# Preparing a graph layer's weights: W1 slices turned one ahead, a few loads moved forward, and part of the products given to GpSimd

## The chip, the cores and the metric

The kernel runs on one core of a Trainium2 chip. A core has five engines that run their own instruction lists in order and wait for one another by semaphores: TensorE (PE, matrix products; its weight loads are shown apart as PEld), VectorE (DVE), ScalarE (ACT), GpSimd (POOL) and SyncE (SP), which here only starts transfers. Transfers (DMA) are started from the lists of SP, ACT and POOL. The metric is the device time of one execution in microseconds (us), taken as the median of several runs.

## The reference, cut to what matters

The program is one block over 1250 rows of 768 numbers: a graph attention layer, a linear attention and a mixture of experts. The change touches only the way in which the weights of the graph layer are prepared. What is computed there:

```
x_norm = layer_norm(layernorm(x), norm_g, norm_b)      # 1250 x 768
h1     = x_norm @ W1                                   # W1: 768 x (4 heads x 192)
s_src1 = (h1 * a_src1).sum(-1);  s_dst1 = (h1 * a_dst1).sum(-1)
out1   = softmax-weighted sum of h1 over the edges, per head, + b1
h2     = out1 @ W2                                     # W2: 768 x (2 heads x 96)
s_src2 = (h2 * a_src2).sum(-1);  s_dst2 = (h2 * a_dst2).sum(-1)
```

All of it is linear between the two softmaxes, so the kernel multiplies the weights together first. `w2x` holds W2 with extra columns: W2 times `a_src2` and times `a_dst2`, summed per head, and the values of `a_src1` and `a_dst1`. `wg` is diag(norm_g) W1 times `w2x`, head by head; `bw` is norm_b W1 times `w2x`. The rows of the graph then only have to be multiplied by `wg`.

## The kernel before, in words

The part in question is the first of the program, and everything else follows it. It is written in one function, `gps_block`, in the pools named ph1.

**Loads.** SP starts W2 (`w2`, L164), W1 in three pieces of two slices each (`w1s`, L170), then `wub` and the edge ends (`ends_i`). POOL starts the ten tiles of x (`acc`, L175); nine of them are held behind the second piece of W1 by a dependency written out by hand (L177). ACT starts the small vectors: four loads into `rb` (L190), `ra` (L191), the two rows of `a2` spread over 96 partitions (L193, L194), `nbb` (norm_b spread likewise, L196), `br` and `sgb`. Each transfer signals one of a few semaphores; a load that takes one whose former load is under way waits for it to land.

**Small transposes.** `turned` (L202) turns `rb` and `ra` on TensorE and copies them out on ACT (`bc`, `gb`).

**w2x** (L213 to L225) on VectorE: it is cleared, W2 is copied in (L216), and for j = 0 (a_src2) and j = 1 (a_dst2) the product of W2 and the spread row is taken in two halves of 96 x 768 (`pr`, L221) and summed along the rows into `w2x` (L224). Two small copies put columns of `bc` in (L225).

**The slices of W1** (loop of L230 over KD = 6 slices k): eight transposes (L235, `p_w1` in PSUM, four to a bank), two copies to `wt` on ACT (L236; two buffers), a product of `wt` with norm_b on VectorE (`wb1`, L238; one buffer) and its sum into a column of `bw1` (L239), the products of `wt` with `w2x` on TensorE (L244) and the eviction to `wg` on ACT, scaled by `gb` (L246).

**After the loop**: the sum `bws` (L249), the products for `bw` (L254), for `bias` (L264, L266) and `b1w2` (L271); the layer norm's statistics of the first tiles (`norm(0)`: `moments`, L141 to L144, and `rsqrt`, L126 to L131); the edge ends are cast on POOL (`ends_f`, L283), turned on TensorE (`pe`, L287) and made into tables on VectorE (`src_f`, `hi`, `lo`, `key`, `rel`, L289 to L301).

**The stage behind it** (L318 to L420) counts edges and multiplies the tiles by `wg`: VectorE writes one-hot tables (`los`, L374; `wide`, L377), TensorE multiplies them (`pc`, L387), and in between turns the normalised rows (`pt`, L406) and multiplies them by `wg` (`ph`, L411). POOL adds `bias` to `acc` (L402).

**What sets the order.** The text is not the order of execution. The build's planner takes the instructions of all engines, with their dependencies and its own idea of durations, and writes one fixed list for each engine; on the chip each engine works its list strictly in order. So layer norm instructions of L141 to L155 and L401 stand among those of the weights on VectorE's list, and which comes first is decided when the program is built. The rotating buffers (`bufs=`) of a pool add waits: a tile's next write waits for the readers of the one it replaces.

Of the kernel before, what the change touches and what calls it, by code (L numbers as in the profile page):

```python
# [8 lines left out]
F32 = mybir.dt.float32  # L9
# [10 lines left out]
P = 128  # L20
# [4 lines left out]
KD = D // P  # L25
# [5 lines left out]
H1, C1 = 4, 192  # L31
H2, C2 = 2, 96
# [17 lines left out]
CO = H2 * (C2 + 1) + 2 * H2  # L50
# [5 lines left out]
def part_bcast(ap, parts, n):  # L56

    return bass.AP(tensor=ap.tensor, offset=ap.offset, ap=[[0, parts], [1, n]])
# [3 lines left out]
def gps_block(ctx: ExitStack, tc: tile.TileContext, x, src, dst, norm_g, norm_b, W1, a_src1, a_dst1, b1,  # L62
              W2, a_src2, a_dst2, b2, Wu, bu, w_qkv, w_proj, b_proj, router_w, w_gate, w_up, w_down,
              ws_gate, ws_up, ws_down, sg_w, sg_b, out):
    nc = tc.nc
# [14 lines left out]
    ident = const.tile([P, P], F32, name="ident")  # L80
# [80 lines left out]
    with tc.tile_pool(name="ph1", bufs=1, reuse_waits="tile") as p1, tc.tile_pool(name="ph1w", bufs=2, reuse_waits="tile") as p1w, \  # L161
            tc.tile_pool(name="ph1ps", bufs=2, space=PSUM, reuse_waits="tile") as ps:
        w2 = p1.tile([C2, 2 * H1, H2 * C2], F32, name="w2")
# [3 lines left out]
        w1s, w1d = [], []  # L167
# [15 lines left out]
        nc.sync.dma_start(ends_i[:, 1, :], dst.rearrange("(r e) -> r e", e=2 * TP))  # L183


        ra = p1.tile([KD, P], F32, name="ra")
        rb = p1.tile([3 * 2 * H1 + H2, C2], F32, name="rb")
        for i, (v, n) in enumerate(((b1, 8), (a_src1, 8), (a_dst1, 8), (b2, 2))):
            v = v if len(v.shape) == 1 else v.rearrange("h c -> (h c)")
            nc.scalar.dma_start(rb[8 * i:8 * i + n, :], v.rearrange("(k p) -> k p", p=C2))  # L190
        nc.scalar.dma_start(ra[0:KD, :], norm_g.rearrange("(k p) -> k p", p=P))  # L191
        a2 = p1.tile([C2, 2, H2 * C2], F32, name="a2")
        nc.scalar.dma_start(a2[:, 0, :], part_bcast(a_src2, C2, H2 * C2))  # L193
        nc.scalar.dma_start(a2[:, 1, :], part_bcast(a_dst2, C2, H2 * C2))  # L194
        nbb = p1.tile([C2, D], F32, name="nbb")
        nc.scalar.dma_start(nbb, part_bcast(norm_b, C2, D))  # L196
        br = p1.tile([2, D], F32, name="br")
        nc.scalar.dma_start(br[0:1, :], bu.rearrange("(o d) -> o d", o=1))
        nc.scalar.dma_start(br[1:2, :], b_proj.rearrange("(o d) -> o d", o=1))
        nc.scalar.dma_start(sgb, part_bcast(sg_b, TP, 1))  # L200

        def turned(rows, n, w, name):  # L202
            pt = ps.tile([P, 4, P], F32, name=f"p_{name}", tag="tr")
            nc.tensor.transpose(pt[:w, 0, :n], rows, ident[:n, :n])
            c = p1.tile([w, n], F32, name=name)
            nc.scalar.copy(c, pt[:w, 0, :n])
            return c

        bc = turned(rb, 3 * 2 * H1 + H2, C2, "bc")
        gb = turned(ra, KD, P, "gb")  # L210


        w2x = p1.tile([C2, 2 * H1, CG], F32, name="w2x")  # L213
# [3 lines left out]
        for j in range(2):  # L217
            o = H2 * (C2 + 1) + j * H2
            for k0 in range(0, 2 * H1, 4):
                pr = p1w.tile([C2, 4, H2, C2], F32, name="pr")  # L220
                nc.vector.tensor_mul(pr, w2[:, k0:k0 + 4].rearrange("p k (h c) -> p k h c", h=H2),  # L221
                                     a2[:, j, :].rearrange("p (h c) -> p h c", h=H2)[:, None].to_broadcast(
                                         [C2, 4, H2, C2]))
                nc.vector.tensor_reduce(w2x[:, k0:k0 + 4, o:o + H2], pr, axis=AX.X, op=ALU.add)  # L224
            nc.vector.tensor_copy(w2x[:, :, CO + j], bc[:, 8 * (j + 1):8 * (j + 2)])  # L225

        bw1 = p1.tile([C2, KD, 2 * H1], F32, name="bw1")
        for k in range(KD):  # L230
            wt = p1w.tile([C2, 2 * H1, P], F32, name="wt")
            for j0 in range(0, 2 * H1, 4):
                pt = ps.tile([P, 4, P], F32, name="p_w1", tag="tr")
                for j in range(4):
                    nc.tensor.transpose(pt[:C2, j, :], w1s[k][:, (j0 + j) * C2:(j0 + j + 1) * C2], ident)  # L235
                nc.scalar.copy(wt[:, j0:j0 + 4, :], pt[:C2, :, :])  # L236
            wb1 = p1w.tile([C2, 2 * H1, P], F32, name="wb1", bufs=1)
            nc.vector.tensor_mul(wb1, wt, nbb[:, None, k * P:(k + 1) * P].to_broadcast([C2, 2 * H1, P]))  # L238
            nc.vector.tensor_reduce(bw1[:, k, :], wb1, axis=AX.X, op=ALU.add)  # L239
            pm = ps.tile([P, 2, 512], F32, name="p_wg", tag="mm", bufs=3)  # L240
            for h in range(H1):
                o = (h % 2) * CG
                for i in range(2):
                    nc.tensor.matmul(pm[:, h // 2, o:o + CG], wt[:, 2 * h + i, :], w2x[:, 2 * h + i, :],  # L244
                                     start=(i == 0), stop=(i == 1))
            nc.scalar.activation(wg[:, k, :].rearrange("p (s c) -> p s c", s=2), pm[:, :, :2 * CG], AF.Copy,  # L246
                                 scale=gb[:, k:k + 1])
        bws = p1.tile([C2, 2 * H1], F32, name="bws")
        nc.vector.tensor_reduce(bws, bw1.rearrange("p k j -> p j k"), axis=AX.X, op=ALU.add)  # L249
        pb = ps.tile([TP, 2, 512], F32, name="pb", tag="mm", bufs=3)  # L250
# [67 lines left out]
    with tc.tile_pool(name="cnt", bufs=1, reuse_waits="tile") as cp, \  # L318
# [74 lines left out]
        for t0 in range(0, NT, 2):  # L393
# [4 lines left out]
            for i, t in enumerate(ts):  # L398
# [4 lines left out]
                for k0 in range(0, KD, 3):  # L403
                    pt = ps.tile([P, 4, P], F32, name="pt", tag="tr")
# [94 lines left out]
    with tc.tile_pool(name="ph2", bufs=1, reuse_waits="tile") as p2:  # L499
# [14 lines left out]
        with tc.tile_pool(name="kvw", bufs=2, side="right", reuse_waits="tile") as p2w, tc.tile_pool(name="kvps", bufs=2, space=PSUM, reuse_waits="tile") as ps:  # L514
# [5 lines left out]
            for pr in range(0, NPAIR, 2):  # L520

                wkv = wkv0
                if pr > 0:
                    wkv = (p2w if pr == 2 else early).tile([P, KD, 2, 2 * P], F32, name=f"wkv{pr}", bufs=1,
                                                           tag="wkv" if pr == 2 else "early")
# [280 lines left out]
    with tc.tile_pool(name="fln", bufs=2, reuse_waits="tile") as pw, tc.tile_pool(name="flnps", bufs=2, space=PSUM, reuse_waits="tile") as ps:  # L806
# [40 lines left out]
        for r in range(2):  # L847
# [5 lines left out]
            f = pw.tile([TP, NT], F32, name=f"r_f{r}", bufs=1)  # L853
# [310 lines left out]
```

## Time and profile before

| | |
|---|---|
| median of 3 runs | 1597.15 us (1594.57 to 1598.87) |
| the profiled execution: its own time | 1597.16 us |
| its span | 1595.1 us |
| granted TensorE clock, mean | 0.985 of full speed |
| busy: PE, PEld | 1525.0 us (96%), 855.7 us (54%) |
| busy: DVE, ACT, POOL | 724.4 us (45%), 367.6 us (23%), 98.1 us (6%) |
| first product of w2x and a W1 slice (L244) starts | 17.71 us |
| first product of the counting stage (L387) starts | 59.62 us |

How to read the views. The timeline has one line for each group of equal instructions in a row: start, busy time, engine, source line, operation, output<-inputs, partitions x elements, count, and in square brackets how long the engine had been idle before and what ended that. Waits are listed as waiting engine and line, what it waited for, and total us, number, longest. A window's line gives for each engine its busy time and the number of instructions, then the granted TensorE clock (PEclk), the share of time that the transfer engines were busy, and GB/s. TensorE works on 32-bit products in two passes, so the trace counts two instructions for one that the program writes; transposes are counted once.

### The profile page before, as it was taken

Reading aid. Unit: us, or ns where it says so; the run is one execution under the profiler, and the core shown is the slowest. Engines: PE = TensorE matmul, PEld = TensorE weight load, DVE = VectorE, ACT = ScalarE, POOL = GpSimd, SP = SyncE. Lnnn points to the kernel's source line nnn. Section 1 sums busy time; section 2 is a strip of 40 time slices with the busy share of each in tenths; the row PEclk is TensorE's granted clock in tenths of the full one; section 3 lists DMA queues with packets and bytes.
Section 4 is the critical chain, followed back from the end, with each engine's and each line's share of the span. In section 5 each row is a group of like instructions: output and inputs, shape, how many; then the busy total and the mean of one; then the engine's idle time right before and its main releaser. Section 6 shows DMA issues by size and latency. Waiting matters only on the chain. (4 is left out here: it accounts for less than half of the span.)

```text
span 1595.1 us, 18670 instructions
## 1 busy us (share of the span) xinstructions
PE 1525.0 (96%) x7143; PEld 855.7 (54%) x7143; DVE 724.4 (45%) x1355; ACT 367.6 (23%) x630; POOL 98.1 (6%) x144
## 2 busy tenths in 40 slices
PE   5999889999999989999999999999999999999986
PEld 5666544444454669896555554444444444444443
DVE  7889639411535359996799651111111111111116
ACT  3222211111101048881276310101111010111100
POOL 2211000000000000000000100000100001000000
PEclk9999989999999999999999999999999999999998
DMA  7100031001201111002121343688888888888727
GB/s 202 40 1 1 2 132 65 7 0 50 63 10 50 40 46 33 33 17 78 33 62 49 108 176 151 218 316 321 301 311 317 317 308 307 307 326 312 265 101 270
DMA packets 92835, 229.18 MB, mean 144 GB/s; under 512 B 5431, under 2 KB 28061, under 8 KB 92742
## 3 DMA queue, kind: packets, MB, share of 16 engines
q1 hardware_dynamic: 84428, 199.30, 35.8%
q0 software_dynamic: 6112, 27.95, 5.0%
q8 instruction: 64, 1.05, 0.3%
q10 hardware_dynamic: 2202, 0.64, 0.2%
q14 instruction: 29, 0.24, 0.0%
HBM read 212.42 MB, written 16.43 MB: 143 GB/s over the span
## 5 line engine op out<-in xcount | busy, mean ns | idle before, releaser
L1012 PE MATMUL pgb<-wg,xT 128*64 128x384 f32 (+1 forms) x1056 | 178.8, 488 | 0.5 <-ACT xT L1019 0.5
L1012 PE MATMUL pdb<-wd,hT 128*64 128x384 f32 (+1 forms) x1056 | 175.1, 488 | 1.4 <-SPq L1092 1.4
L1012 PE MATMUL pub<-wu,xT 128*64 128x384 f32 (+1 forms) x1056 | 174.0, 486 | 0.0
L533 PE MATMUL pp<-wkv,xnT 128*125 128x512 f32 x360 | 160.8, 595 | 0.1
L615 PE MATMUL pa<-G,u 125*125 125x199 f32 x800 | 140.4, 336 | 11.2 <-DVE h L623 6.0
L615 PEld LDWEIGHTS pa<-G,u 125*125 125x125 f32 x800 | 135.6, 189 | 16.2 <-issue 7.2
L1012 PEld LDWEIGHTS pub<-wu,xT 128*64 128x64 f32 x1056 | 75.7, 137 | 94.5 <-issue 94.5
L1012 PEld LDWEIGHTS pdb<-wd,hT 128*64 128x64 f32 x1056 | 74.6, 137 | 91.6 <-issue 87.0
L1012 PEld LDWEIGHTS pgb<-wg,xT 128*64 128x64 f32 x1056 | 73.7, 137 | 90.7 <-issue 89.8
L533 PEld LDWEIGHTS pp<-wkv,xnT 128*125 128x125 f32 x360 | 65.6, 189 | 73.1 <-issue 72.7
L1031 DVE TENSOR_TENSOR h<-h,pgb 128x384 f32<-128x384 f32 x44 | 24.4, 554 | 171.7 <-ACT h L1030 171.7
L1042 DVE COPY y<-pdb 128x768 f32<-128x768 f32 x22 | 21.1, 958 | 178.8 <-PE pdb L1012 178.8
L411 PE MATMUL ph<-wg,xnT 128*125 128x400 f32 x240 | 99.6, 521 | 2.5 <-PEq L425 2.4
L598 DVE SCALAR_TENSOR_TENSOR u<-ea,cntT 125x625 f32<-125x625 f32 x120 | 93.9, 805 | 12.6 <-PE pa L615 8.0
L595 ACT ACTIVATE eb<-r,g_ss 125x625 f32<-125x625 f32 x120 | 95.0, 816 | 20.3 <-DVE ea L596 20.3
L596 DVE TENSOR_TENSOR ea<-ea,eb 125x625 f32<-125x625 f32 x120 | 94.0, 805 | 8.2 <-ACT ea L593 5.4
L480 DVE CUSTOM_DVE_ANT_0 junk<-ssb,absent 125x1250 bf16<-125x1250 f32 x60 | 87.8, 1463 | 11.7 <-DMA ssb<-g_srow_d 10.4
L1030 ACT ACTIVATE h<-pgb 128x384 f32<-128x384 f32 x44 | 21.6, 491 | 307.6 <-PE pgb L1012 307.6
L563 PE MATMUL pq<-xnT,wq 128*128 128x500 f32 (+1 forms) x216 | 82.6, 527 | 4.6 <-DMA wq<-in_L_mix_w_qkv_dram 4.5
L1036 DVE TENSOR_TENSOR h<-h,pub 128x384 f32<-128x384 f32 x44 | 24.4, 554 | 134.4 <-PE pub L1012 134.4
L715 PE MATMUL pu<-wu,xnT 128*125 128x384 f32 x240 | 82.1, 487 | 1.3 <-DVE acc L720 1.3
L576 PE MATMUL pu<-wp,at 128*125 128x384 f32 x240 | 80.4, 488 | 1.0 <-DVE acc L579 1.0
(267 smaller groups left out, 1666.9 us busy)
## 6 DMA issues: line engine op xcount, KB each, us to landing
wg<-in_L_ffn_w_gate_dram SPq DMA_DIRECT2D x22, 2304.0 KB, 8.4
wu<-in_L_ffn_w_up_dram SPq DMA_DIRECT2D x22, 2304.0 KB, 10.4
wd<-in_L_ffn_w_down_dram SPq DMA_DIRECT2D x22, 2304.0 KB, 9.6
yg<-ys SPq DMA_DIRECT2D x10, 768.0 KB, 9.4
r<-g_rrow_d SPq DMA_DIRECT2D x12, 625.0 KB, 4.0
wq<-in_L_mix_w_qkv_dram SPq DMA_DIRECT2D x18, 384.0 KB, 3.5
wkv<-in_L_mix_w_qkv_dram SPq DMA_DIRECT2D x6, 768.0 KB, 12.3
acc<-in_x_dram POOLq DMA_DIRECT2D x10, 375.0 KB, 10.6
```

What stands on the lines that cost most here:

```text
L411: nc.tensor.matmul(ph[:, :2 * CG], xnT[:, k, tok], wg[:, k, s * 2 * CG:(s + 1) * 2 * CG], start=(k == 0), stop=(k == KD - 1))
L480: nc.vector.tensor_tensor_reduce(out=junk, in0=self.ssb[:TP], in1=absent[:, dt, :], scale=1.0, scalar=-3.0e38, op0=ALU.add, op1=ALU.max, a ...
L533: nc.tensor.matmul(pp, xnT[:, k, tok], wkv[:, k, :, :], start=(k == 0), stop=(k == KD - 1))
L563: nc.tensor.matmul(pq[:, :qw], wq[:, k, :], xnT[:, k, tok], start=(k == 0), stop=(k == KD - 1))
L576: nc.tensor.matmul(pu[:, s, :HALF], at[:, k, i * TP:(i + 1) * TP], wp[:, k, s * HALF:(s + 1) * HALF], start=(k == 0), stop=(k == KD - 1))
L595: nc.scalar.activation(eb, r[:TP, 1, :], AF.Exp, bias=ss02[:, st, h:h + 1])
L596: nc.vector.tensor_max(ea, ea, eb)
L598: nc.vector.scalar_tensor_tensor(u, ea, 1.0, cntT[:, st, half * W:(half + 1) * W], op0=ALU.min, op1=ALU.mult)
L615: nc.tensor.matmul(pa[i][:, :CO + 1], u[:, i * TP:(i + 1) * TP], G[:, st, h, :CO + 1], start=(st == 0), stop=(st == NT - 1))
L715: nc.tensor.matmul(pu[:, :HALF], xnT[:, k, t * TP:(t + 1) * TP], wus[s][:, k, :], start=(k == 0), stop=(k == KD - 1))
L1012: nc.tensor.matmul(pt[part, :HALF], rows[:, k, part], w[:, k, s * HALF:(s + 1) * HALF], start=(k == 0), stop=(k == KD - 1))
L1031: nc.vector.tensor_mul(h, h, pgs[s][:, :HALF])
```

## The change

Five edits, all in the first part of the program.

1. The two loads of `a2` on ACT's list come first, ahead of `rb` and `ra`.
2. A one-element copy on ACT (`idle`) from `ident` is added behind the loads; ACT's first load of its function table goes with it.
3. The transposes and the two copies of a slice become a function `split(k)`. Slice 0 is turned ahead of `bc` and `gb`; in the loop, slice k+1 is turned ahead of the products of slice k.
4. The `pr` products with j = 1, the two copies of L225 and the six `wb1` products (L238) go from VectorE to GpSimd. `pr` has a name for each j, so each j has two buffers of its own.
5. Nothing is taken out: the same numbers are computed, and the sums stay on VectorE.

```diff
+        a2 = p1.tile([C2, 2, H2 * C2], F32, name="a2")
+        nc.scalar.dma_start(a2[:, 0, :], part_bcast(a_src2, C2, H2 * C2))
+        nc.scalar.dma_start(a2[:, 1, :], part_bcast(a_dst2, C2, H2 * C2))
         ra = p1.tile([KD, P], F32, name="ra")
         rb = p1.tile([3 * 2 * H1 + H2, C2], F32, name="rb")
...
         nc.scalar.dma_start(ra[0:KD, :], norm_g.rearrange("(k p) -> k p", p=P))
-        a2 = p1.tile([C2, 2, H2 * C2], F32, name="a2")
-        nc.scalar.dma_start(a2[:, 0, :], part_bcast(a_src2, C2, H2 * C2))
-        nc.scalar.dma_start(a2[:, 1, :], part_bcast(a_dst2, C2, H2 * C2))
...
+        idle = p1.tile([1, 1], F32, name="idle")
+        nc.scalar.copy(idle, ident[0:1, 0:1])
...
+        def split(k):
+            wt = p1w.tile([C2, 2 * H1, P], F32, name="wt")
+            for j0 in range(0, 2 * H1, 4):
+                pt = ps.tile([P, 4, P], F32, name="p_w1", tag="tr")
+                for j in range(4):
+                    nc.tensor.transpose(pt[:C2, j, :], w1s[k][:, (j0 + j) * C2:(j0 + j + 1) * C2], ident)
+                nc.scalar.copy(wt[:, j0:j0 + 4, :], pt[:C2, :, :])
+            return wt
+
+        wt = split(0)
         bc = turned(rb, 3 * 2 * H1 + H2, C2, "bc")
         gb = turned(ra, KD, P, "gb")
...
-                pr = p1w.tile([C2, 4, H2, C2], F32, name="pr")
-                nc.vector.tensor_mul(pr, w2[:, k0:k0 + 4].rearrange("p k (h c) -> p k h c", h=H2),
-                                     a2[:, j, :].rearrange("p (h c) -> p h c", h=H2)[:, None].to_broadcast(
-                                         [C2, 4, H2, C2]))
+                pr = p1w.tile([C2, 4, H2, C2], F32, name=f"pr{j}")
+                (nc.vector, nc.gpsimd)[j].tensor_mul(pr, w2[:, k0:k0 + 4].rearrange("p k (h c) -> p k h c", h=H2),
+                                                     a2[:, j, :].rearrange("p (h c) -> p h c", h=H2)[:, None].to_broadcast(
+                                                         [C2, 4, H2, C2]))
                 nc.vector.tensor_reduce(w2x[:, k0:k0 + 4, o:o + H2], pr, axis=AX.X, op=ALU.add)
-            nc.vector.tensor_copy(w2x[:, :, CO + j], bc[:, 8 * (j + 1):8 * (j + 2)])
+            nc.gpsimd.tensor_copy(w2x[:, :, CO + j], bc[:, 8 * (j + 1):8 * (j + 2)])
...
         for k in range(KD):
-            wt = p1w.tile([C2, 2 * H1, P], F32, name="wt")
-            for j0 in range(0, 2 * H1, 4):
-                pt = ps.tile([P, 4, P], F32, name="p_w1", tag="tr")
-                for j in range(4):
-                    nc.tensor.transpose(pt[:C2, j, :], w1s[k][:, (j0 + j) * C2:(j0 + j + 1) * C2], ident)
-                nc.scalar.copy(wt[:, j0:j0 + 4, :], pt[:C2, :, :])
+            after = split(k + 1) if k + 1 < KD else None
             wb1 = p1w.tile([C2, 2 * H1, P], F32, name="wb1", bufs=1)
-            nc.vector.tensor_mul(wb1, wt, nbb[:, None, k * P:(k + 1) * P].to_broadcast([C2, 2 * H1, P]))
+            nc.gpsimd.tensor_mul(wb1, wt, nbb[:, None, k * P:(k + 1) * P].to_broadcast([C2, 2 * H1, P]))
             nc.vector.tensor_reduce(bw1[:, k, :], wb1, axis=AX.X, op=ALU.add)
             pm = ps.tile([P, 2, 512], F32, name="p_wg", tag="mm", bufs=3)
...
+            wt = after
```

## The prediction

> **What bounds the kernel now.** The page first: it says which engine sets the time as a whole.
>
> ```profile
> PE 1525.0 (96%) x7143; PEld 855.7 (54%) x7143; DVE 724.4 (45%) x1355; ACT 367.6 (23%) x630; POOL 98.1 (6%) x144
> ```
>
> TensorE is busy nearly throughout, so a late start of its long stages is a late end, unless they have slack. The change lies before 60 us, so the timeline of that stretch comes next, engine by engine. TensorE:
>
> ```profile
> 17.71 5.70 PE L244 MATMUL p_wg<-w2x,wt 96*128 96x200 f32 x16 [4.29 <-DVE w2x L225]
> ...
> 24.06 2.95 PE L244 MATMUL p_wg<-w2x,wt 96*128 96x200 f32 x16
> ...
> 41.87 2.98 PE L244 MATMUL p_wg<-w2x,wt 96*128 96x200 f32 x16 [0.61 <-ACT wt L236]
> 44.69 0.56 PE L287 MATMUL pe<-ident,ends_f 80*125 80x80 f32 x4
> 45.58 2.97 PE L254 MATMUL pb<-w2x,bws 96*125 96x200 f32 x16 [0.34 <-DVE bws L249]
> 48.48 0.91 PE L264 MATMUL pb<-br,ones 2*125 2x384 f32 x2
> ...
> 54.41 4.78 PE L271 MATMUL pb<-w2x,bc 96*125 96x198 f32 x16
> ...
> 59.62 0.41 PE L387 MATMUL pc<-wide,los 125*125 125x500 f16 x1
> ```
>
> The first products wait for `w2x` until 17.71. From there TensorE hardly rests. The edge transposes `pe` stand ahead of `bw`, `bias` and `b1w2`, so VectorE makes its tables while TensorE does 13.5 us of those. VectorE:
>
> ```profile
> 17.50 0.16 DVE L225 COPY w2x<-bc 96x8 f32<-96x8 f32 x1
> 17.57 1.21 DVE L238 TENSOR_TENSOR wb<-wt,nbb 96x1024 f32<-96x1024 f32 x1
> 22.22 0.56 DVE L141 BATCH_NORM_STATS2 ln_st<-acc 125x6 f32<-125x384 f32 x1 [3.44 <-DMA acc<-in_x_dram]
> ...
> 51.56 1.19 DVE L374 TENSOR_TENSOR los<-lo,steps 125x1000 f16<-125x1000 f16 x1
> ```
>
> `w2x` was whole at 17.66, before the layer norm's first tile of x landed at 22.2. VectorE's chain from `pe` to the first tables takes from 45.07 to 53.2, all under TensorE's work. POOL is free, but starts its last x load only when an earlier one lands:
>
> ```profile
> 22.48 0.53 POOL L175 DMA_DIRECT2D acc<-in_x_dram x1 [3.61 <-DMA acc<-in_x_dram]
> ```
>
> **The change, part by part.** Each engine's list of the changed kernel is fixed when it is built, and can be read without a run; the same listing of the kernel before agrees with its trace. VectorE's, shortened:
>
> ```
> copies of W2 into w2x; pr(j=0) x2; their sums x2
> layer norm: 13 statistics (tiles 0 to 6), 2 xn, some 20 small ones
> sums of pr(j=1) x2            <- w2x is whole only here
> sum of wb1 slice 0; 4 small norm ones; ...; sum of slice 1; ...; the rest of the norm; sums of slices 2 to 5; bws
> src_f, dst_f, hi ... rel, los, wide
> ```
>
> TensorE's: transposes of slices 0, 1, 2, then the products of slices 0 and 1, transposes of 3, products of 2, and so on to products of 4 and 5; `bw`, `bias`, `b1w2`; only then the transposes `pe`, and the counting stage. POOL's: all x loads, then a small copy, `pr`(j=1) x2, a copy, `wb1` 0, `ones`, the cast of the edges, `base`, `wb1` 1 to 5. From the first hundred entries on, every list is the one of before. So I follow the first 85 us.
>
> *Loads and ACT.* The a rows landed at 10.50; at the head of ACT's list they can be there before the copies of W2 are done (6.07 + 1.03 = 7.1). Two products (1.82) and two sums (1.80) end at 10.7, and at 14.1 if the rows land no earlier. Either is hidden: VectorE then waits for x until 22.2. The third load on ACT's list, `rb`, releases the second piece of W1 as now (issued at 7.66), so I leave x at 22.2, give or take 1.5 (three tiles' share of the queue). The table load (1.28) moves off ACT's start; it too is hidden by that wait, as are `bc`, `gb` and slices 0 to 2 on TensorE.
>
> *VectorE up to w2x.* 13 statistics at 0.48 apart (6.2), 2 xn at 0.62 (1.2), 20 small ones at 0.11 (2.2): 9.6 us. GpSimd now runs `pr`, `pr`, `wb1` in that time, and that is not free:
>
> ```profile
> 137.09 1.81 POOL L402 TENSOR_TENSOR acc<-acc,bias 125x768 f32<-125x768 f32 x1 [1.66 <-DVE xn L401]
> ...
> 137.48 1.44 DVE L128 TENSOR_TENSOR ln_rs<-ln_rs 125x2 f32<-125x2 f32 x1
> ```
>
> A two-number product that takes 0.15 elsewhere ends with GpSimd's instruction, at 138.9. The bounds here are 0 and the three products whole (6.2); lining the lists up, one norm product meets the end of `pr` (0.4) and one the start of `wb1` (2.2): 2.6. The sums of j=1 start at 22.2 + 9.6 + 2.6 = 34.4, and two of 0.9 end at 36.2. GpSimd's side is earlier: 23.0 + 0.2 + 2 x 1.9 (from L402, 768 long) = 27.0. First product: 36.3 instead of 17.71, **+18.6**.
>
> *The slices.* Before, 17.71 to 44.69 is 27.0. Now slice 0 at half clock again (5.7), slice 1 (2.85), three times transposes and products (1.04 + 2.85), slice 5 (2.85): 23.1, ended at 59.4. That is the edit's gain, 3.9: the four waits of 0.61 for ACT and two slices' transposes done early. But `bw` also waits for the sums. A `wb1` on GpSimd has no row; L402 gives 2.34 ns an element on average, so 2.4 for 1024. VectorE's own 1.20 and L402's slowest, 2.16 x 1024/768 = 2.9, are the ends; I take 2.4, as the same operation on the same engine. With one buffer the chain is product, sum, product: 2.4 + 1.2 + 0.15. Slice 0's sum ends at 37.4, slice 1's product at 40.1, slice 2's at 46.3; the rest of the norm holds the sum of 2 until 47.9 to 49.1; three rounds more end at 60.3, `bws` at 60.6. So `bw` starts at 60.6 instead of 45.58: **+15.0** now stands.
>
> *The rest of the weights.* `bw`, `bias`, `b1w2` take 13.55 from 45.58 to 59.13, and I keep that: 74.2. Part of it ran at half clock, although TensorE had been busy for long:
>
> ```profile
> 50.00:52.00 2.00, 2.00 (x6) 0.78 (x5) 1.93 (x8) 0.00 (x0) 0.00 (x0) 0.88 0.00 0
> 52.00:54.00 2.00, 2.00 (x4) 1.07 (x4) 2.00 (x7) 0.00 (x0) 0.00 (x0) 0.50 0.00 0
> ```
>
> The Trainium skill ("TensorE: Matmul & The Clock Gate", section "What's actually happening") has the clock fall after an idle window of about 3.4 us and stay full under work; these rows do not follow it. By that rule this part would be some 3 us shorter (L271 at L254's 2.97, not 4.78, the later L266 at 1.55) and the forecast 1618. I keep the rows, since the same instructions come in the same order.
>
> *The edges.* `pe` takes 0.56, to 74.8, and VectorE's chain is uncovered: `src_f` and `dst_f` 0.6, nine `hi` 2.9, `lo`, `key`, `lo16`, `rel` 1.1, `los` 1.2, `off` and the first `wide` 0.6: 6.4. First counting product at 81.3 instead of 59.62, **+21.7**. Behind it stand `off`, the second `wide` and `offs` (0.9) before `po`, six `pt` and ACT's copy, which lay partly ahead of it before: `ph` comes 2.3 after it, not 1.12, **+1.2**. TensorE was idle for 6.5; before 17.7, 4.3 idle us were followed by 6.4 at half clock. Ends 0 and 3.2; I take **+1.5**.
>
> GpSimd's `rest` and the `wide` clears follow `wb1` 5 (59 to 63), its `bias` additions `bias` (70.4 to 74.2): both before they are needed. SP's queue has the load of `ys` and then `wkv` behind `rest`; `wkv` is read some 130 us later.
>
> *No cover later.* From 60 to 180 TensorE's own idle waits sum to some 5 us, so the delay passes on whole. Sum: 21.7 + 1.2 + 1.5 = **24.4**. The profiled execution's own time is 1597.16 (span 1595.1), the median 1597.15, the same: 1621.
>
> **The rivals.**
> A: the delay with its discounts. If GpSimd and VectorE don't meet, the walk is 4 shorter; if the clock stays full, 3 in the weights and 1.5 after; x 1.5 earlier. All: +14.4, 1611.5. For it: the lock's row is one instruction; against: a clear repeat of the half clock is likely.
> B: GpSimd becomes the bound. If a product with a spread operand takes 3.4 instead of 2.4, four rounds and the locks add 7; with x later and the clock's 3.2: 1630 or a little over. Against: L402 keeps within 1.8 to 2.16.
> C, faster: the relief counts. VectorE loses 9.4 us (six `wb1` at 1.2, two `pr` at 0.95, two copies), the a rows come 3.4 earlier, the slices gain 3.9: 1590. It decides at one point, whether `w2x` is whole by 17.7. That needs x at 10.7 and the norm in front in under 5 us; its rows say 9.6, and POOL issues x at 14.66. With x at 10.7 the same walk still gives +10.
> D: no change, 1597. The counting stage would have to absorb 24; its waits are 5.
>
> **How the numbers follow.** The main case (1616 to 1626) 0.62, A (1609 to 1616) 0.18, B (1626 to 1632) 0.13, C 0.05, D 0.02. Less than 0.3% (4.8 us) can't be told from no change here: faster 0.05, same 0.03, slower 0.92. The range, 1611 to 1630, takes in most of A and B.
>
> **What the profile after would show.** Right: VectorE idle from about 11 to 22 for `acc`; the first L254 (the old L244) near 36, released by VectorE's `w2x`; TensorE idle some 6 us ahead of the first count product near 81; transposes one slice ahead with no wait for ACT. Wrong: a first product before 30, `wb1` far from 2.4, or the counting stage shorter than before by several us.

## The result, and the profile after

The changed kernel takes 1620.76 us (median of 4 runs, 1618.2 to 1623.82), the kernel before 1596.7 us beside it (1594.57 to 1598.87): a ratio of 1.0152, 95% interval 1.0136 to 1.0169, so 24 us slower. The profiled execution took 1623.82 us, with a span of 1622.1 (before: 1597.16 and 1595.1).

The page of the changed kernel, busy time by engine:

```profile
PE 1530.7 (94%) x7143; PEld 858.2 (53%) x7143; DVE 723.7 (45%) x1345; ACT 368.1 (23%) x631; POOL 113.9 (7%) x154
```

TensorE does the same 7143 instructions and is busy for 5.7 us more in a span that is 27.0 longer. So the loss is mostly idle time. VectorE, which was to be relieved, shows 723.7 against 724.4: almost all of the 9.4 us of products that left it came back, 8.8 of it in three instructions on two numbers (4.71, 2.31 and 2.20 us, where their like take 0.15 each).

The timeline of TensorE in the changed kernel (start, busy time, engine, line, operation, count, idle time before and its releaser):

```profile
15.13 3.70 PE L218 MATMUL p_w<-ident,w 128*96 128x128 f32 x16
36.46 8.08 PE L254 MATMUL p_wg<-w2x,wt 96*128 96x200 f32 x32 [17.62 <-DVE w2x L238]
...
52.42 5.58 PE L254 MATMUL p_wg<-w2x,wt 96*128 96x200 f32 x32
60.49 4.33 PE L265 MATMUL pb<-w2x,bws 96*125 96x200 f32 x16 [2.50 <-DVE offs L343]
...
73.46 3.86 PE L282 MATMUL pb<-w2x,bc 96*125 96x198 f32 x16
77.16 0.56 PE L298 MATMUL pe<-ident,ends_f 80*125 80x80 f32 x4
83.75 0.68 PE L398 MATMUL pc<-wide,los 125*125 125x500 f16 x1 [6.03 <-DVE wide L388]
...
86.29 2.88 PE L422 MATMUL ph<-wg,xnT 128*125 128x400 f32 x4
```

Three slices are turned by 18.8, and then TensorE waits 17.62 us for `w2x`. It waits again for `bws` (the releaser named is `offs`, the next small instruction on VectorE), and a third time, 6.03 us, for the edge tables, because `pe` now stands behind the weights. The answering starts before were 17.71 (first product), 45.58 (`bw`), 59.62 (`pc`) and 60.74 (`ph`).

The timeline of VectorE in the changed kernel:

```profile
22.40 1.48 DVE L141 BATCH_NORM_STATS2 ln_st<-acc 125x6 f32<-125x384 f32 x3 [10.08 <-DMA acc<-in_x_dram]
...
25.32 4.71 DVE L144 TENSOR_SCALAR ln_ve<-ln_mv 125x2 f32<-125x2 f32 x1
...
35.37 1.80 DVE L238 TENSOR_REDUCE w2x<-pr 96x8 f32<-96x768 f32 x2
...
38.50 2.31 DVE L129 TENSOR_TENSOR ln_rs<-ln_rs,ln_ve 125x2 f32<-125x2 f32 x1
...
55.13 1.22 DVE L249 TENSOR_REDUCE bw<-wb 96x8 f32<-96x1024 f32 x1 [2.53 <-POOL wb L248]
...
60.11 0.23 DVE L260 TENSOR_REDUCE bws<-bw 96x8 f32<-96x48 f32 x1
...
77.54 0.33 DVE L300 COPY src_f<-pe 125x160 f32<-125x160 f32 x1 [17.19 <-PE pe L298]
```

VectorE waits 10.08 us for x with two short sums of `w2x` still to do, works through the norm, and only then does those sums. From 48.8 on it waits about 2.5 us for each `wb1` of GpSimd, and then 17.19 us for `pe`: idle while TensorE does the weights, and TensorE is idle next while VectorE makes the tables. GpSimd, same view:

```profile
23.34 3.56 POOL L235 TENSOR_TENSOR pr<-w,a 96x768 f32<-96x768 f32 x2
26.84 0.19 POOL L239 COPY w2x<-bc 96x8 f32<-96x8 f32 x1
26.99 2.33 POOL L248 TENSOR_TENSOR wb<-wt,nbb 96x1024 f32<-96x1024 f32 x1
29.27 0.19 POOL L271 MEMSET ones<- 128x125 f32 x1
29.41 0.59 POOL L294 CAST ends_f<-ends_i 80x500 f32<-80x500 int32 x1
29.97 0.30 POOL L310 IOTA base<- 125x160 f32 x1
...
56.48 2.35 POOL L248 TENSOR_TENSOR wb<-wt,nbb 96x1024 f32<-96x1024 f32 x1 [1.39 <-DVE bw L249]
```

GpSimd's products with a2 start at 23.34, behind the last load of x, although VectorE had taken W2 at 7.83 and the first a row at 8.78. They end at 26.9. So, as an estimate from these rows, the first product could not have started before about 27 even with its sums next on VectorE's list: that is 9 of the 18.75 us that it is late, and the norm with the stall in it is the rest. No run moved the sums alone. The windows of the changed kernel (PE, PEld, DVE, ACT, POOL busy, then the granted clock):

```profile
66.00:68.00 2.00, 2.00 (x4) 1.06 (x4) 0.00 (x0) 0.00 (x0) 0.00 (x0) 0.50 0.00 0
72.00:74.00 2.00, 2.00 (x5) 1.20 (x4) 0.00 (x0) 0.30 (x1) 0.00 (x0) 0.50 0.00 0
```

The granted clock is 0.50 from about 62 to 75, over most of the weights' products, although TensorE works without a pause there.

### The profile page after: what moved, and what is told of

Its sections match the earlier page's. It is cut to its first block, busy times and chain, and to the rows that moved or that the text cites. A ratio compares the mean times of both kernels' runs of the same rounds, so it can differ in the third digit from the quotient of the medians.

```text
span 1622.1 us, 18682 instructions
## 1 busy us (share of the span) xinstructions
PE 1530.7 (94%) x7143; PEld 858.2 (53%) x7143; DVE 723.7 (45%) x1345; ACT 368.1 (23%) x631; POOL 113.9 (7%) x154
## 5 line engine op out<-in xcount | busy, mean ns | idle before, releaser
L1042 DVE TENSOR_TENSOR h<-h,pgb 128x384 f32<-128x384 f32 x44 | 24.4, 554 | 171.7 <-ACT h L1041 171.7
L1047 DVE TENSOR_TENSOR h<-h,pub 128x384 f32<-128x384 f32 x44 | 24.4, 554 | 134.4 <-PE pub L1023 134.4
```

What stands on the lines that cost most here:

```text
L1042: nc.vector.tensor_mul(h, h, pgs[s][:, :HALF])
```

## The experiments

The theories. **L** (the prediction's): the lists decide. On VectorE the sums that need GpSimd stand behind the norm, which waits for x, and on TensorE `pe` stands behind the weights. Rivals: **G**, GpSimd's products and their chain are slow in themselves; **O**, turning slices ahead, with the order that it brings, is the main cost; **W**, the late `w2x` alone is the whole cost. "After" is the changed kernel. Ratios are against the kernel before, run beside each, with 95% intervals. All the kernels compute the whole of the reference.

### The parts of the GpSimd share

e1: the products with a2 and the two copies back on VectorE; `wb1` stays on GpSimd.

```diff
-                (nc.vector, nc.gpsimd)[j].tensor_mul(pr, ...
+                nc.vector.tensor_mul(pr, ...
-            nc.gpsimd.tensor_copy(w2x[:, :, CO + j], ...
+            nc.vector.tensor_copy(w2x[:, :, CO + j], ...
```

> The changed kernel with pr (j=1) and the two small copies back on VectorE; only the six wb1 products stay on GpSimd. Theory L (the lists): the loss comes from where the layer norm stands on VectorE's list, once ahead of the sums that finish w2x, once ahead of the sums of wb1, and from the edge transposes standing last. Here w2x no longer waits for the norm: first product at 17 to 18, but the sums of wb1 still stand behind the norm, so the bw products start near 53 (60.5 in the changed kernel, 45.6 before): 1610 to 1615. Theory G (the engine): GpSimd's products are slow in themselves and the product-sum chain of wb1 on one buffer sets the time; with that chain kept, bw stays near 60 and the time at 1617 to 1622. Theory O (turning ahead): the late edge transposes are the main cost: 1618 to 1621.

Measured: 1615.89 us, 1.0126 [1.0099, 1.0153]. The time lies between the ranges of L and G, 0.9 above the one and 1.1 below the other. The first product starts at 16.87, but `bw` only at 54.20.

e2: the reverse, `wb1` back on VectorE, `pr` stays on GpSimd.

```diff
-            nc.gpsimd.tensor_mul(wb1, ...
+            nc.vector.tensor_mul(wb1, ...
```

> The changed kernel with the six wb1 products back on VectorE; only pr (j=1) and the two copies stay on GpSimd. L: w2x is still behind the norm, first product at 35 to 37, slices end near 57, bw near 58: 1615 to 1620. G: the slow chain is gone, bw at 46 to 50: 1606 to 1611. O: 1618 to 1621.

Measured: 1611.84 us, 1.0098 [1.0081, 1.0115]. First product at 32.82, `bw` at 53.63. The time is a miss for L, 3.2 below its range and 0.8 above G's. Both starts came earlier than L said, and the products of `bw`, `bias` and `b1w2` ran at full clock (10.0 us, 16.67 in after).

e3: both edits, nothing on GpSimd.

> The changed kernel with all products back on VectorE; a rows first, turning ahead and the early table load stay. L: first product near 16, bw at 41 to 45, then the late edge transposes leave VectorE's 6.4 us of tables uncovered and the clock at half after it: 1599 to 1604, a little slower than before. G: 1590 to 1596, faster than before, as nothing on GpSimd is left. O: the late transposes are the main cost and remain: 1612 to 1618.

Measured: 1605.01 us, 1.0045 [1.0031, 1.006], 1 us above L's range. First product at 17.30, `bw` at 41.13.

e4: the kernel before with the GpSimd share alone (edit 4 of the change).

> The kernel before with only the share given to GpSimd (pr j=1, two copies, six wb1); loads and turning as before. L: w2x behind the norm, first product near 36; half of the edge transposes also moves behind the weights when the lists are made, so the tables are uncovered here too: 1616 to 1623, all of the loss. G: the same, 1616 to 1623. O: turning ahead is not in it, so 1597 to 1603.

Measured: 1613.76 us, 1.011 [1.0093, 1.0127]. That is 2.2 us below the range of L and G. First product at 35.20 after a wait of 20.02, `bw` at 61.63. Half of `pe` did go behind the weights: two of its instructions start at 60.01, two at 71.76.

What follows: the GpSimd share costs 1.07% of the time taken out of after (1.0152 less 1.0045), and 1.10% put into before. The halves don't add up: taken out alone, one gains 0.26% and the other 0.54%. Either half leaves a late `bw`, one through `w2x`, the other through the sums of `wb1`. So W alone falls (e1 has `w2x` early and keeps most of the loss), and O can't be the main cost (e3 is under a third of the loss). G is still open here.

One caution. The products of `bw`, `bias` and `b1w2` took 10.0 to 17.9 us in these kernels, by the granted clock (table in the last section), and that is in every one of these times. The start of `bw` lies ahead of it and says the same: 60.49 in after, 54.20 and 53.63 with one half taken out, 41.13 with both, and 61.63 with the share put into before (45.58).

### The edges' place

e6: after, with the edge block (`ends_f`, `pe`, `src_f` to `rel`) written ahead of `bws`. e7: e3 with the same move.

```diff
+        ends_f = ...; nc.gpsimd.tensor_copy(ends_f, ends_i)
+        ... pe ... src_f, dst_f ... hi, lo, key, rel
         bws = p1.tile([C2, 2 * H1], F32, name="bws")
```

> The changed kernel with the cast, the transposes pe and the tables of the edges moved in the text ahead of bws, so that pe stands ahead of the bw products on TensorE's list; all else as in the changed kernel. Theory L: first product and bw stay near 36 and 60; the 6 us in front of the first count product, its half clock (about 2) and the 1.2 of order go: 1610 to 1614. Rival W (the late w2x alone costs, the tables would have been hidden anyway): 1618 to 1622.

Measured: 1611.17 us, 1.0093 [1.0061, 1.0124]; `pc` waits for no table any more.

> The changed kernel with nothing on GpSimd and pe early: what is left is the a rows first, the table load moved and the turning ahead. L: first product near 17, bw near 41, the first ph product near 59 to 60 (60.7 before, 66.9 with pe late): 1592 to 1598, the same as before or a little faster. Rival (turning ahead harms in itself, by VectorE's and ACT's order): 1601 to 1606.

Measured: 1594.99 us, 0.9983 [0.9969, 0.9996]. TensorE's timeline of e3:

```profile
17.30 3.74 PE L254 MATMUL p_wg<-w2x,wt 96*128 96x200 f32 x16
...
57.80 0.56 PE L298 MATMUL pe<-ident,ends_f 80*125 80x80 f32 x4
64.36 0.68 PE L398 MATMUL pc<-wide,los 125*125 125x500 f16 x1 [6.00 <-DVE wide L388]
```

and of e7:

```profile
16.98 3.83 PE L254 MATMUL p_wg<-w2x,wt 96*128 96x200 f32 x16
...
39.77 0.56 PE L266 MATMUL pe<-ident,ends_f 80*125 80x80 f32 x4
...
54.85 0.41 PE L399 MATMUL pc<-wide,los 125*125 125x500 f16 x1
```

The 6.00 of waiting is gone and `pc` comes 9.5 us earlier; the weights took 4.8 us less by the clock (16.7 against 11.9 us), and `bw` started 1.3 later. The late `pe` is worth 0.59% in after (e6) and 0.62% without GpSimd (e7), some 9.5 to 10 us. In e6 the weights took as long as in after (16.8 and 16.7), so its figure is free of that clock; e7's is not. And the parts nearly add up: 1.10% for the GpSimd share put into before (e4), 0.62% for the late `pe` (e3 less e7), and a gain of 0.17% for the rest of the change (e7) make 1.55%, against 1.52% measured. This is no proof of a clean split: e4 has half of the late `pe` in it (TensorE waited 2.75 us for the tables), and the clock in the weights differs from kernel to kernel. `pe` went behind the weights in e3, where GpSimd does nothing, and not in e5 below; so something in the rest of the change moves it: the slices turned ahead, the small copy on ACT, or the added buffers of `pr`. These were not parted, and in e4 the GpSimd share alone moved half of it.

### GpSimd in itself, or its place in the lists

e8: after, with the loads of x written behind the products with a2, so that GpSimd takes those first. e9: e8 with the edge block of e6. e14: e9 with `wb1` back on VectorE.

```diff
-        for t in range(NT):            # the loads of x
-            get = nc.gpsimd.dma_start(...)
...
             nc.gpsimd.tensor_copy(w2x[:, :, CO + j], ...
+        for t in range(NT):
+            get = nc.gpsimd.dma_start(...)
         bw1 = p1.tile([C2, KD, 2 * H1], F32, name="bw1")
```

> The changed kernel with the loads of x written behind the pr products, so that GpSimd takes its two pr products before it starts the loads of x; wb1 stays on GpSimd, pe late. L, whose second part says that the sums of wb1 are behind the norm as well: first product near 17 instead of 36, but bw no earlier than 54 to 60, so 1612 to 1621. Rival W: the late w2x is the whole cost, 1598 to 1604.

Measured: 1616.46 us, 1.0129 [1.0106, 1.0151]. The first product starts at 15.73, 20.7 us earlier than in after, and the time gains only 0.23%.

> The changed kernel with both repairs and the whole GpSimd share kept: loads of x written behind the pr products, edges ahead of bws. L: first product near 15.7; the sums of wb1 still stand behind the norm on VectorE, so bw starts near 57 as in e8; tables lie beside the weights, so no wait of 6 us: 1605 to 1609, still a loss. If it is 1600 or less, the sums behind the norm do not matter and late w2x with late pe was all. If it is 1614 or more, the two repairs do not add up.

Measured: 1610.01 us, 1.0086 [1.0069, 1.0102], 1 us above what L gave. The timeline of e9, TensorE, ACT and VectorE together:

```profile
15.89 5.09 PE L255 MATMUL p_wg<-w2x,wt 96*128 96x200 f32 x16 [0.46 <-POOL w2x L234]
...
32.85 0.20 ACT L126 ACTIVATE ln_rs<-ve 125x2 f32<-125x2 f32 x1 [3.83 <-DVE ve L155]
...
33.05 1.05 ACT L214 COPY wt<-p_w 96x512 f32<-96x512 f32 x2
33.67 1.94 PE L213 MATMUL p_w<-ident,w 128*96 128x128 f32 x8 [9.11 <-ACT wt L214]
...
35.41 1.20 DVE L250 TENSOR_REDUCE bw<-wb 96x8 f32<-96x1024 f32 x1
...
54.48 1.22 DVE L250 TENSOR_REDUCE bw<-wb 96x8 f32<-96x1024 f32 x1 [2.51 <-POOL wb L249]
...
56.02 5.50 PE L289 MATMUL pb<-w2x,bws 96*125 96x200 f32 x16 [5.01 <-DVE offs L345]
```

The first `wb1` was done by GpSimd at 27.4, and its sum ran at 35.41, behind the norm; with one buffer the next `wb1` waited for that sum. From there the chain of product, sum, product takes 3.75 us a slice, and `bws` is done at 56. Besides, the norm stands in a third list: ACT's two square roots of it (L126) are ahead of the copy of slice 2's `wt` and waited for VectorE until 32.85, so TensorE stood 9.11 us in the middle of the slices. The prediction had not looked at that list; in after nothing came of it, since `w2x` was later still.

> As e9, but the wb1 products are back on VectorE; GpSimd keeps half of pr and the two copies. On the list of VectorE no sum that needs GpSimd stands behind the norm any more. L: first product near 15.7, bw near 42 as in e7, 1594 to 1601: GpSimd's half of pr costs nothing when nothing stands behind it. G (GpSimd slow in itself): 1607 or more, as in e2 (1611.8) less the gain of an early pe only.

Measured: 1594.03 us, 0.9982 [0.9972, 0.9992], the lowest median of all, though 0.18% is less than the 0.3% that the prediction calls the least that can be told. TensorE's timeline of e14:

```profile
16.83 5.70 PE L255 MATMUL p_wg<-w2x,wt 96*128 96x200 f32 x16 [2.02 <-POOL w2x L234]
...
42.95 4.65 PE L289 MATMUL pb<-w2x,bws 96*125 96x200 f32 x16 [2.83 <-DVE bws L284]
...
55.35 0.75 PE L400 MATMUL pc<-wide,los 125*125 125x500 f16 x3
```

Here GpSimd still does half of `pr` (1.91 and 1.80 us for its two products, about twice VectorE's 0.9), and it costs nothing: e14 and e7, which gives GpSimd nothing, stand at 0.9982 and 0.9983. VectorE's own two products took 3.43 us beside them instead of 1.82, and still the first product starts at 16.83 (16.98 in e7). The same two products at the place that the change gave them on GpSimd's list cost 0.53% (e2 less e3): 8.5 us by the ratios, 6.8 by the medians. There `bw` starts 12.5 us later, and 6.6 of it came back by the clock in the weights (10.0 against 16.7). For them G falls and L holds. For `wb1` the two can't be parted wholly: its first sum is late by the list (L), but the chain behind it, 3.75 a slice, is GpSimd's own pace with one buffer (G). A kernel with early sums and `wb1` on GpSimd was not run.

### The loads of a2

e5: the kernel before with the two rows of a2 first on ACT's list and nothing else; the other engines' lists are those of before.

> The kernel before with the two rows of a2 at the head of ACT's list and nothing else changed (edit 1 alone); every other list is the one of before. All theories: the products with a2 start with the copies of W2 done, 1.5 to 3.4 us earlier, but the last column of w2x waits for bc, which comes from rb, now loaded behind a2; first product 16.5 to 17.7 instead of 17.71. 1593 to 1598, no difference that can be told. Above 1600 would mean that the order of the loads has a share in the loss.

Measured: 1599.08 us, 1.0014 [1.0001, 1.0027]: 1.1 us above the range, and less than the 0.3% that can be told. The products with a2 did come earlier, and the first product started at 16.50 instead of 17.71. By the start of `bw` nothing of that was left (46.29 against 45.58), since TensorE waited 2.84 us for a `wt` at 29.1; the last section shows what came behind it.

### Two tries at a faster kernel

e11: e7 with the products of `bw` behind `bias` and `b1w2`, so that TensorE doesn't wait for `bws`. e13: the same with the order `b1w2`, `bw`, `bias`.

```diff
-        bws = ...;  pb <- bws, w2x;  nc.scalar.copy(bw, ...)
         pb2 ... bias;  pb3 ... b1w2
+        bws = ...;  pb <- bws, w2x;  nc.scalar.copy(bw, ...)
         ahead = norm(0)
```

> As the kernel with nothing on GpSimd and pe early, and with the bw products behind those of bias and b1w2, so that TensorE has no wait for VectorE's sums in front of them. If the half clock in this part follows an idle stretch of TensorE (2.2 us for the sums with nothing on GpSimd and pe late), it goes with the wait: 1586 to 1592, faster than before. If the half clock comes from these products themselves, as before, where TensorE did not idle: 1592 to 1597.

Measured: 1596.81 us, 1.0001 [0.9992, 1.0011]; the faster kernel was missed. The time lies in the second range, but the condition of the first is what the trace shows: the wait for `bws` went, the weights ran at full clock throughout and were done at 49.7. The gain was lost behind them, as the tables weren't ready: TensorE waited 4.63 us for `offs`. Two of VectorE's instructions (1.77 and 1.89 us where their like take 0.15 and 0.3) stood beside GpSimd's additions of `bias`, which now came earlier. VectorE and GpSimd in e11:

```profile
45.29 3.57 POOL L416 TENSOR_TENSOR acc<-acc,bias 125x768 f32<-125x768 f32 x2 [3.54 <-ACT bias L293]
45.35 1.77 DVE L130 TENSOR_SCALAR ln_rs<-ln_rs 125x2 f32<-125x2 f32 x1
...
47.15 1.89 DVE L274 SCALAR_TENSOR_TENSOR hi<-src_f,hi 125x160 f32<-125x160 f32 x1
```

> As e11 (nothing on GpSimd, pe first), with the weights in the order b1w2, bw, bias, so that GpSimd's additions of bias to acc start only near 50 instead of 45.3 and VectorE's tables are not held by them. If the two held instructions (1.77 and 1.89) were e11's loss: offs 3 to 4 us earlier, first count product near 51 to 52, 1590 to 1594, below the kernel before. If the norm's instructions among the tables were the loss: 1595 to 1598 as e11.

Measured: 1595.47 us, 0.9997 [0.9986, 1.0007], in the second range. GpSimd's additions start at 57.3, behind the tables up to `offs`, but in this order the slices waited twice for `wt` (2.35 and 2.17 us) and ended 5 us later than in e11, so its expectation could not be tested cleanly. Neither of them beats e7 or e14.

## Why the prediction was right

It said 1621 and 1620.76 was measured, and the account holds in its main steps. (Its sum, 1597.16 and 24.4, is 1621.6.) Its terms against the trace of after:

| step | predicted | measured |
|---|---|---|
| x lands, VectorE goes on | 22.2 | 22.40 |
| VectorE comes to the sums of `w2x` | 34.4 | 35.37 |
| first product | 36.3 | 36.46 |
| slices end | 59.4 | 58.00 |
| `wb1` on GpSimd, one | 2.4 | 2.33 to 2.36 |
| `bws` done, `bw` starts | 60.6 | 60.49 |
| `bw`, `bias`, `b1w2` together | 13.55 | 16.67 |
| from `pe`'s start to `pc` | 7.1 | 6.59 |
| `pc` against before | +21.7 | +24.1 |
| `ph` behind it, more than before | +1.2 | +1.4 |
| half clock after it, rest of the span | +1.5 | +1.45 |

**Right, and shown by runs.** `w2x` behind the norm: the first product is 0.2 us from the forecast, by errors that cancel (below), and e8 brings it to 15.73. The chain of `wb1` that holds `bw`: 0.1 us off, with a step of 3.73 where 3.75 was said; e9 shows that it acts with `w2x` early too. The uncovered tables: e6 and e7 take them away and get 9.4 to 10 us back, in e7 with the help of the clock. No cover later: `ph` is 25.55 late, and the span 27.0 longer.

**Mis-sized: the weights.** "`bw`, `bias`, `b1w2` take 13.55 [...] and I keep that" is the term that failed. It measured 16.67, 3.1 more, because almost all of it ran at half clock, where before only the later part did. At full clock the same instructions take 10.0 (e2). The reason given for keeping the row, the same instructions in the same order, does not hold. The rule that the prediction set against it (the Trainium skill, "TensorE: Matmul & The Clock Gate", section "What's actually happening") erred to the other side: it would have the clock full under work and made the forecast 1618.

**Mis-sized, and cancelled.** The stall beside GpSimd was 4.6, not 2.6, and the norm itself 8.4 instead of 9.6: 0.8 more together. It did not reach TensorE, because the first product needs only the first of the two sums of j = 1, which ended 0.9 before the second; the prediction made it wait for both. The slices ended 1.4 earlier than said, without effect, since `bw` waited for `bws` anyway. By these terms the loss in the profiled execution is 2.6 above the sum (27.0 against 24.4), and that execution stands 3 us above the median of its runs. These two set each other off, so it is luck that the number came within 1 us.

**The rivals.** A (the discounts) needed no meeting of GpSimd and VectorE and a full clock, and neither came. B (GpSimd the bound at 3.4 a product) fell with 2.35, though the chain does bound the weights' sums. C (faster) needed `w2x` by 17.7; e8 and e9 have it by 15.9 and are still slower than before, so its point of decision was set too low: the sums of `wb1` must be early too. With `wb1` back on VectorE and `pe` early, in e14, it is faster by 0.18%, and not by the 7 us of C. D (no change) fell with the 24 us.

## What to carry to other kernels

When work moves to a slower but free engine, look at what stands ahead of it on the new engine's list and ahead of its consumer on the consumer's, not only at the price of the operation. Two products of 1.9 us cost nothing measurable ahead of the loads of x, with their sums ahead of the norm, and some 7 to 8.5 us behind both. Compare the built order of all engines before and after an edit; here `pe`, which no edit names, went behind the weights and cost some 9.5 us, and writing its block earlier got that back. And when two parts each hold the same successor, taking one out shows only a part of its cost, so take out both.

## What was not expected of the hardware

**A short instruction held over several of the other engine's.** L144 in after, which adds a constant to two numbers, took 4.71 us, until GpSimd had done a product, a copy, another product, a memset and a cast in a row (25.32 to 30.0). In e14, with GpSimd idle at that moment, it took 0.15:

```profile
31.46 0.15 DVE L144 TENSOR_SCALAR ln_ve<-ln_mv 125x2 f32<-125x2 f32 x1
```

So in these rows the turn did not come with the end of one instruction. What does end the wait isn't clear from them: in after it ended with the cast, though the iota (L310) followed at once at 29.97, and in e4 the same instruction took 5.03 us, to 28.86, where the iota ended at 28.83. The statistics (L141) beside the same run were not held. The Trainium skill ("SBUF — State Buffer", section "Who interferes with whom") has the two engines share a pair of ports, taken for a whole instruction, and lists this operation among those that can take it; the row agrees, with the addition that several instructions in a row hold it through. That is my reading of the rows; no run put a gap between GpSimd's instructions.

**The same products at 10.0 to 17.9 us.** `bw`, `bias` and `b1w2`, with the idle time of TensorE just ahead of them and the length:

| kernel | idle ahead, us | length, us |
|---|---|---|
| e2, e4, e5 | 0, 1.28, 0.34 | 10.0, 10.1, 10.2 |
| e7, e14, e8 | 2.11, 2.83, 5.49 | 11.9, 11.9, 12.2 |
| before | 0.34 | 13.55 |
| e9, e3, after, e6, e1 | 5.01, 2.15, 2.50, 2.01, 5.85 | 16.1, 16.7, 16.7, 16.8, 17.9 |

The granted clock accounts for it, and it is not set by the idle time alone: e5 and before have 0.34 and differ by 3.3, e7 and e3 have 2.1 and differ by 4.8. The clock-gate rule named above fits neither the half clock under unbroken work nor these pairs. Each length is that of one execution, and other executions of one kernel differ in their mean granted clock along with their time: in e3 0.986 at 1598.35 us and 0.981 at 1608.16, in e7 0.991 at 1589.45 and 0.986 at 1597.16. So a row of this table may belong to the execution and not to the kernel. What sets the clock stays open.

**A shorter part that bought nothing.** In e5 the weights took 3.3 us less than before, and `ph` still came 0.9 later (61.68). TensorE, VectorE and GpSimd in e5:

```profile
54.51 4.22 DVE L377 TENSOR_SCALAR wide<-steps,rel 125x500 f16<-125x500 f16 x4
54.82 3.75 POOL L402 TENSOR_TENSOR acc<-acc,bias 125x768 f32<-125x768 f32 x2 [8.23 <-ACT bias L268]
...
59.95 0.87 PE L406 MATMUL pt<-ident,xn 125*128 125x125 f32 x3 [2.53 <-DVE off_i L336]
```

`bias` was ready sooner, GpSimd's additions met VectorE's `wide` (4.22 for four, 1.12 in e11 where GpSimd was idle), and TensorE waited 2.53 us for what stood behind them.
